# Graph message passing on one core: rows of x picked by TensorE in more steps, a third picked tile in every fourth step, and the edge bias put into PSUM by ScalarE

## The chip, the cores and the metric

The kernel runs on one core of a Trainium2 chip. The metric is the device time of one execution in microseconds (us); lower is better.

## The reference, cut to what matters

```python
# N = 6250 nodes, 64 channels, 4 heads of D = 16; 206250 edges, sorted by destination
Qh = (x @ Wq.T + bq).reshape(n, H, D)
Kh = (x @ Wk.T + bk).reshape(n, H, D)
Vh = (x @ Wv.T + bv).reshape(n, H, D)
Ee = (edge_attr @ We.T + be).reshape(-1, H, D)
score = (Kh[src] * Qh[dst] * (1.0 / np.sqrt(D)) * Ee).sum(-1)
score = jnp.exp(jnp.clip(score, -5.0, 5.0))
msg = Vh[src] * score[..., None]
wV = jax.ops.segment_sum(msg, dst, num_segments=n)
x = _layernorm(x + wV.reshape(n, H * D), axis=-1)
```

Two things are random access: the rows of K and V at `src`, and the rows of Q and of the output at `dst`. Since the edges are sorted by destination, the latter move slowly along the node axis; the sources are anywhere.

## The kernel before

**Tiling.** The edges are padded to 1612 tiles of 128. Eight tiles make a group (202 groups). The main loop has 105 steps: 97 of two groups (16 tiles), then eight of one group (8 tiles, the last 4). All tensors of a step lie with the edge of a tile on the partition.

**Prologue.** TensorE makes the tables: `kv_tab` (K and V of each node, f32, in HBM) and `q3_tab` (Q in three bf16 parts whose sum is the f32 value). The first four groups don't wait for `kv_tab`: GpSimd gathers rows of x (L230) and TensorE turns and multiplies them (L375 to L384). Then GpSimd starts gathering rows of `kv_tab`, one indirect DMA for each tile of 128 edges (L402, `gather_kv`), into one of five buffers `kvs`.

**Three ways to a K/V row.** Most tiles are gathered by L402. In each sixth step one tile comes by 128 single-row DMAs of the SP queue (L544, `rk`). And in steps 4 to 94 two tiles are *picked*: the last two tiles of the step after the next are made by TensorE. For a picked tile, ScalarE makes 50*column - source (`far`, L466), TensorE transposes it into the PSUM tile `small` (L471), VectorE compares that with block numbers and so makes 50 one-hot matrices of 128x128 in bf16 (`hot`, L481, in two halves of 25), and TensorE multiplies each with a block of `parts` (x in three bf16 parts; L491, 25 matmuls a half) and adds them up in PSUM (`pick`). VectorE adds the three parts (`xp`, L498), TensorE transposes, ScalarE copies, TensorE multiplies with the K and V weights (L513, L515), and ScalarE copies the result into `kvs` (L516). `parts` is made in the first steps of the loop from x in HBM, by `table_parts` and `table_parts_rest`.

**A step.** The schedule is written out by hand; each engine runs its instructions in program order. In step s, for step s+1: `spread` (L555) puts the destinations' offsets over the partitions, ScalarE makes one-hot rows `to` in two instructions (L572 Square, L577 Relu), `queries` (L595) multiplies them with the window of Q, `edges` (L388, L391) multiplies the edge attributes with their weights, and `onehot_edges` (L585) makes the one-hot columns. L388 is a matmul of three rows that starts each accumulation with the bias `be`, one for each group. For step s itself: two products on VectorE (L602 with Q, L603 with the edge values `pe`), the sum over each head (L609), the clip (L611), exp on ScalarE (L612), the message (L619). The message goes into three bf16 parts: ScalarE copies the first (L622), TensorE subtracts it in PSUM (L630, `minus`), ScalarE copies the next (L632), twice. For step s-1: `sums` (L638) multiplies the parts with the one-hot columns, and `add` (L652) adds the result to a ring of accumulators. When a block of 128 nodes is complete, in about every second step, VectorE closes it (L668 to L678), and later normalises it (L688). All the little PSUM tiles of a step (the turned sources, the scores, the sums) share the one tile `small`.

Of the kernel before, what the change touches and what calls it, by code (L numbers as in the profile page):

```python
# [40 lines left out]
TB = 8  # L41
M0 = 4
# [21 lines left out]
LAST = NS - 8 - 3  # L64


def picks_in(s):
    return M0 <= s <= LAST

# [5 lines left out]
COLUMN = 2 * G - 3  # L75
# [27 lines left out]
def tile_gnn(ctx: ExitStack, tc: tile.TileContext, x, xT, wT, bias, beT, weT, eT, src, dst, dst_rows,  # L103
# [52 lines left out]
    bkv_p = consts.tile([3, G // 2, 2 * C], BF16, name="bkv_p")  # L156
    minus_b = consts.tile([P, P], BF16, name="minus_b")
# [26 lines left out]
    with tc.tile_pool(name="nodes", bufs=1) as nodes, \  # L184
# [36 lines left out]
        nc.sync.dma_start(be_sb, beT.to_broadcast([3, C]))  # L221
        nc.vector.memset(we_sb, 0.0)
# [147 lines left out]
        for g in range(XG):  # L370
            for h in range(2):
                tp = npsum.tile([P, 2, P], F32, name="tp", bufs=2)
                for u in range(2):
                    j = 4 * h + 2 * u
                    nc.tensor.transpose(tp[:, u, :],  # L375
                                        XS[g][:, j:j + 2, :].rearrange("p j c -> p (j c)"), ident)
                xe = nodes.tile([P, 2, P], F32, name="xe", bufs=2)
                nc.scalar.activation(xe, tp, AF.Copy)
                pv = npsum.tile([P, 4, 2 * C], F32, name="pv", bufs=2)
                nc.tensor.matmul(pv, ones_b, bkv_p, start=True, stop=False, skip_group_check=True)  # L380
                for u in range(2):
                    nc.tensor.matmul(pv[:, 2 * u:2 * u + 2, :], xe[:, u, :], wkv, start=False,
                                     stop=u == 1, skip_group_check=True)
                nc.scalar.activation(kv_of(g)[:, 4 * h:4 * h + 4, :], pv, AF.Copy)  # L384

    def edge_values(pe, et, n):

        nc.tensor.matmul(pe[:, :n, :], ones_b, be_p[:, :n, :], start=True, stop=False,  # L388
                         skip_group_check=True)
        for u in range(n // 2):  # L390
            nc.tensor.matmul(pe[:, 2 * u:2 * u + 2, :], et[:, u, :], we_sb, start=False,  # L391
                             stop=u == n // 2 - 1, skip_group_check=True)
# [13 lines left out]
    for g in range(XG, 2 * KVB - 2):  # L406
        for j in range(G):
            gather_kv(g, j)
# [3 lines left out]
    with tc.If(rv == 0) as branch:  # L412

        with tc.tile_pool(name="work", bufs=2) as work, \
# [5 lines left out]
            col, from0, from1 = (small[:, i * C:(i + 1) * C].bitcast(BF16) for i in range(3))  # L420
            from_b = from0, from1
            score_all = small[:, 3 * C:3 * C + 2 * G * H]
            pa = small[:, 4 * C:7 * C].rearrange("p (i c) -> p i c", i=3)
            nc.tensor.transpose(col, row_b[:, 0:1].to_broadcast([P, P]), ident_b)

            parts = accp.tile([P, NB, 3, C], BF16, name="parts")
            nc.vector.memset(parts, 0.0)
            NX = N // NB
            x_v = x.rearrange("(p b) c -> p b c", p=NX)
            n_picks = LAST - M0 + 1  # L430
            src_f = accp.tile([P, n_picks, 2], F32, name="src_f")
            t0 = (M0 + 3) * 2 * G - 2
            for i in range(2):
                nc.vector.tensor_copy(src_f[:, :, i],
                                      src_i[:, t0 + i:t0 + i + 2 * G * (n_picks - 1) + 1:2 * G])
            pick = fixed.tile([P, 4 * P], F32, name="pick")
            rows3 = pick[:, :6 * C].rearrange("p (k i c) -> p k i c", k=2, i=3)
            HOT, FAR, X = {}, {}, {}
# [5 lines left out]
            def table_parts(b):  # L444

                n = min(TB, NB - b)
                raw = work.tile([P, TB, C], F32, name="raw", bufs=1)
                nc.sync.dma_start(raw[:NX, :n], x_v[:, b:b + n, :])
                rest = pick[:NX, :n * C].rearrange("p (b c) -> p b c", b=n)
                nc.scalar.activation(rest, raw[:NX, :n], AF.Copy)  # L450
                nc.scalar.activation(parts[:NX, b:b + n, 0], raw[:NX, :n], AF.Copy)
                return rest

            def table_parts_rest(b, rest):
                n = min(TB, NB - b)
                nc.vector.tensor_sub(rest, rest, parts[:NX, b:b + n, 0])
                nc.scalar.activation(parts[:NX, b:b + n, 1], rest, AF.Copy)
                nc.vector.tensor_sub(parts[:NX, b:b + n, 2], rest, parts[:NX, b:b + n, 1])

            def sources(s, i):  # L460

                if picks_in(s):
                    FAR[s, i] = work.tile([P, P], BF16, name="far")
                    nc.scalar.activation(FAR[s, i], row50, AF.Identity,  # L466
                                         bias=src_f[:, s - M0, i:i + 1], scale=-1.0)

            def sources_turned(s, i):
                if picks_in(s):  # L470
                    nc.tensor.transpose(from_b[i], FAR.pop((s, i)), ident_b)  # L471
# [4 lines left out]
            def hots(s, i, h):  # L476

                if picks_in(s):
                    HOT[s, i, h] = work.tile([P, NB // 2, P], BF16, name="hot", bufs=4)
                    shape = [P, NB // 2, P // 2, 2]  # L480
                    nc.vector.tensor_tensor(  # L481
                        HOT[s, i, h].rearrange("p b (a c) -> p b a c", c=2),
                        pairs(from_b[i])[:, None].to_broadcast(shape),
                        block2[:, blocks(h), None, :].to_broadcast(shape), op=OP.is_equal)

            def picks(s, i, h):
                if picks_in(s):
                    hot = HOT.pop((s, i, h))
                    for k in range(NB // 2):
                        b = h * NB // 2 + k  # L490
                        nc.tensor.matmul(rows3[:, i], hot[:, k, :], parts[:, b], start=b == 0,  # L491
                                         stop=b == NB - 1)

            def picked(s):

                if picks_in(s):
                    xp = work.tile([P, 2, C], F32, name="xp")
                    nc.vector.tensor_reduce(xp, rows3.rearrange("p k i c -> p k c i"), axis=AX.X,  # L498
                                            op=OP.add)
                    X[s] = xp  # L500

            def picked_turned(s):
                if picks_in(s):
                    room = psum.tile([P, G, P], F32, name="pb")
                    nc.tensor.transpose(room[:, 0, :], X[s].rearrange("p k c -> p (k c)"), ident)
                    xe = work.tile([P, P], F32, name="xe")
                    nc.scalar.activation(xe, room[:, 0, :], AF.Copy)
                    X[s] = xe, room[:, 4:6, :]

            def picked_kv(s):  # L510
                if picks_in(s):
                    xe, kv = X.pop(s)
                    nc.tensor.matmul(kv, ones_b, bkv_p[:, :2], start=True, stop=False,  # L513
                                     skip_group_check=True)
                    nc.tensor.matmul(kv, xe, wkv, start=False, stop=True, skip_group_check=True)  # L515
                    nc.scalar.activation(kvs[(s + 2) % KVB][:, 2 * G - 2:, :], kv, AF.Copy)  # L516

            def gather(s):
                for g in groups_of(s):
                    for j in range(tiles_of(g)):  # L520
                        if is_rowed(s) and (g - STEPS[s][0]) * G + j == COLUMN:
                            continue
                        if not picks_in(s - 2) or g == STEPS[s][0] or j < G - 2:
# [36 lines left out]
            def edges(s, k):  # L560

                g = STEPS[s][0] + k
                if k == 0:
                    PE[s] = psum.tile([P, 2 * G, C], F32, name="pe")
                edge_values(PE[s][:, k * G:(k + 1) * G], ET[g], tiles_of(g))
# [134 lines left out]
            closed, scaled, normed = 0, 0, 0  # L700
            keys(0)
# [5 lines left out]
            onehot_edges(0)  # L707
            for s in range(NS):
# [14 lines left out]
                sources_turned(s, 1)  # L723
                sources_turned(s + 1, 0)
                if nexts[1:]:
                    onehot_rows(nexts[1], spread(nexts[1]))
                making = [b for b in range(s * 2 * TB, (s + 1) * 2 * TB, TB) if b < NB]
                if making:
                    rest = table_parts(making[0])
                prod = products(s)  # L730
                picked(s - 1)
                if more:
                    edges(s + 1, 0)
                picks(s, 0, 0)
                score = scores(s, prod)
                if nexts[1:]:
                    onehot_rows_rest(nexts[1])
# [5 lines left out]
                picked_turned(s - 1)  # L743
                if nexts[1:]:
                    edges(s + 1, 1)
                minus(s, msg, 0)
                hots(s, 1, 0)
                picks(s, 0, 1)
                minus(s, msg, 1)
                picked_kv(s - 1)  # L750
# [4 lines left out]
                hots(s, 1, 1)  # L755
                picks(s, 1, 0)
                sources(s + 1, 1)
                sources(s + 2, 0)
                if s + 1 < NS:
# [6 lines left out]
                picks(s, 1, 1)  # L766
                hots(s + 1, 0, 0)
                hots(s + 1, 0, 1)
                if more:
# [13 lines left out]
                for i, b in enumerate(making):  # L783
                    if i:
                        rest = table_parts(b)
                    table_parts_rest(b, rest)
# [12 lines left out]
    with branch.Else():  # L799

        sums = [dram.tile([NR, C], F32, name=f"sums{i}") for i in range(TABLES)]
        with tc.tile_pool(name="gconsts", bufs=1) as gc, \
                tc.tile_pool(name="gloads", bufs=3) as loads, \
                tc.tile_pool(name="ggath", bufs=4) as gath, \
# [28 lines left out]
            def gather(g, j):  # L833
# [3 lines left out]
                if g >= 2 * KVB - 2:  # L837
# [11 lines left out]
            def compute(g):  # L849
# [33 lines left out]
                AGG[g] = work.tile([P, G, C], F32, name="agg", bufs=3)  # L883
# [79 lines left out]
```

## Time and profile before

| | |
|---|---|
| median of 3 runs | 1790.13 us (1790.07 to 1792.62) |
| profiled execution, its own time | 1789.88 us |
| its span, first to last instruction | 1788.0 us |
| mean granted TensorE clock | 0.951 |
| PE busy | 1638.5 us (92%) |
| VectorE (DVE) busy | 1481.6 us (83%) |
| GpSimd (POOL) busy | 1337.4 us (75%) |
| ScalarE (ACT) busy | 914.0 us (51%) |
| share of the chain that ended last | PE 38%, POOL 29%, issue 14%, DVE 13%, DMA 4% |

How to read the lines of the profile: a group's line has source line, engine, operation, output<-inputs, shapes and count, then busy us and mean ns of one, then the idle time of the engine ahead of them and what ended it. A timeline's line has start and duration in us, engine, line, operation and count, and in brackets the engine's idle time before it. A window's line has start:end, length, busy us (and instructions) of PE, PEld (weight loads), DVE, ACT and POOL, the granted TensorE clock, the DMA share and GB/s. POOL's busy time leaves out the 0.30 us between one gather and the next in which it issues. Matmuls are pipelined: the duration of one overlaps the next, so that the distance of starts is what a matmul costs.

### The profile page before, as it was taken

What the parts mean: (1) busy time and instruction counts of PE and PEld (TensorE: products, weight loads), DVE (VectorE), ACT (ScalarE), POOL (GpSimd) and SP (SyncE); (2) the same over time, 40 slices, a digit from 0 to 9 for tenths busy, and PEclk for the clock granted to TensorE, in tenths of its full rate; (3) what the DMA queues carried; (4) which work ended last, traced back from release to release, by engine and by line L of the source; (5) the groups of instructions that cost most, each with busy time, mean ns of one, the idle gap of its engine ahead of it and who ended that gap; (6) DMA issues with size and microseconds to landing.
All of it is one profiled execution on the core that took longest, in us unless ns stands there. A gap on an engine that the chain in (4) does not pass through costs nothing.

```text
span 1788.0 us, 44286 instructions
## 1 busy us (share of the span) xinstructions
PE 1638.5 (92%) x15751; PEld 1369.6 (77%) x15751; DVE 1481.6 (83%) x1695; ACT 914.0 (51%) x1328; POOL 1337.4 (75%) x1427
## 2 busy tenths in 40 slices
PE   8978999999999998999999899999989998999864
PEld 8647888888888787787887778777877887787632
DVE  6459999999998898888889888888988888898654
ACT  3465555555554464454455445455544554455443
POOL 7777777777777777777777777777777777777774
PEclk9968999999999999999999999999999999999855
DMA  7443333333333333332333333323332333333331
GB/s 221 132 121 84 90 93 94 93 94 92 93 81 94 93 86 89 92 94 80 93 93 81 93 81 93 92 81 99 87 93 80 94 93 81 93 90 81 91 80 44
DMA packets 109970, 166.71 MB, mean 93 GB/s; under 512 B 69196, under 2 KB 71452, under 8 KB 109626
## 3 DMA queue, kind: packets, MB, share of 16 engines
q0 software_dynamic: 45280, 91.78, 19.4%
q1 hardware_dynamic: 64074, 71.01, 14.1%
q8 instruction: 125, 2.05, 0.5%
q10 hardware_dynamic: 384, 1.00, 0.3%
q14 instruction: 107, 0.88, 0.2%
HBM read 156.33 MB, written 7.33 MB: 92 GB/s over the span
## 4 chain that ended last, share of the span: by engine, by line
PE 38%; POOL 29%; issue 14%; DVE 13%; DMA 4%; ACT 3%; DVEq 0%; SPq 0%; POOLq 0%; ACTq 0%
POOL kv L402 29%; PE pick L491 18%; PE pe L391 5%; DVE hot L481 5%; DMA kv<-kv_tab,src_i 3%; PE pq L630 2%; PE small L638 2%; DVE prod L603 2%; DVE prod L602 2%; PE pb L555 2%; PE pe L388 2%; PE pb L515 1%; PE pq L595 1%; DVE pq L619 1%; PE ps L350 1%
## 5 line engine op out<-in xcount | busy, mean ns | idle before, releaser
L402 POOL DMA_INDIRECT kv<-kv_tab,src_i x1383 | 1305.3, 944 | 421.7 <-issue 399.8
L491 PE MATMUL pick<-parts,hot 128*128 128x192 bf16 x9100 | 828.3, 249 | 0.0
L491 PEld LDWEIGHTS <-hot 128*128 128x128 bf16 x9100 | 771.7, 99 | 38.1
L481 DVE TENSOR_TENSOR hot<-small,block 128x3200 bf16<-128x3200 bf16 x364 | 645.3, 1813 | 0.4 <-PE pick L491 0.4
L572 ACT ACTIVATE to<-pb,minus_row 126x1024 bf16<-126x1024 f32 x202 | 222.7, 1102 | 371.0 <-PE pb L555 367.2
L632 ACT ACTIVATE msg<-pq 128x1024 bf16<-128x1024 f32 (+2 forms) x210 | 207.6, 989 | 222.3 <-PE pq L630 222.3
L391 PEld LDWEIGHTS pe<-we_sb,et 128*128 128x128 f32 x1612 | 209.7, 203 | 133.4 <-issue 95.3
L602 DVE TENSOR_TENSOR prod<-kv,pq 128x1024 f32<-128x1024 f32 (+2 forms) x105 | 123.5, 1176 | 169.3 <-DMA kv<-kv_tab,src_i 52.0
L391 PE MATMUL pe<-we_sb,et 128*128 128x128 f32 x1612 | 250.3, 302 | 0.0
L577 ACT ACTIVATE to<-to,one_p 126x1024 bf16<-126x1024 bf16 x202 | 230.6, 1142 | 3.5
L638 PEld LDWEIGHTS <-of 128*128 128x128 bf16 x1612 | 145.3, 102 | 31.1 <-issue 7.9
L638 PE MATMUL small<-msg,of 128*128 128x192 bf16 x1612 | 161.9, 257 | 0.5 <-ACT msg L632 0.5
L388 PE MATMUL pe<-be_p,ones_b 3*128 3x512 bf16 x202 | 79.7, 395 | 86.3 <-DVE prod L603 86.1
L630 PE MATMUL pq<-msg,minus_b 128*128 128x512 bf16 x404 | 128.0, 396 | 33.1 <-ACT msg L622 19.5
L622 ACT ACTIVATE msg<-pq 128x1024 bf16<-128x1024 f32 (+2 forms) x105 | 103.8, 989 | 96.8 <-DVE pq L619 96.8
L609 DVE TENSOR_REDUCE small<-prod 128x64 f32<-128x1024 f32 (+2 forms) x105 | 123.6, 1177 | 14.5 <-PE small L471 8.8
L555 PE MATMUL pb<-key_rows,ident_b 112*128 112x512 bf16 x403 | 127.9, 400 | 2.8 <-ACT to L572 2.8
L603 DVE TENSOR_TENSOR prod<-prod,pe 128x1024 f32<-128x1024 f32 (+2 forms) x105 | 123.6, 1177 | 3.6
L619 DVE TENSOR_TENSOR pq<-kv,small 128x1024 f32<-128x1024 f32 (+2 forms) x105 | 123.4, 1175 | 1.4 <-ACT small L612 1.4
L585 DVE TENSOR_TENSOR of<-small,key 128x2048 bf16<-128x2048 bf16 (+2 forms) x105 | 122.9, 1171 | 0.3
L595 PEld LDWEIGHTS <-to 126*128 126x128 bf16 x1612 | 63.5, 101 | 25.3 <-issue 25.1
L612 ACT ACTIVATE small<-small 128x64 f32<-128x64 f32 (+2 forms) x105 | 21.7, 207 | 111.1 <-DVE small L611 109.2
(129 smaller groups left out, 996.4 us busy)
## 6 DMA issues: line engine op xcount, KB each, us to landing
et<-in_eT SPq DMA_DIRECT2D x100, 512.0 KB
rk<-kv_tab SPq DMA_DIRECT2D x1920, 0.5 KB
kv<-kv_tab,src_i POOLq DMA_INDIRECT x1383
qw<-q_tab SPq DMA_DIRECT2D x202, 15.8 KB
kv_tab<-kv_sb SPq DMA_DIRECT2D x5, 640.0 KB
q_tab<-q SPq DMA_DIRECT2D x5, 480.0 KB
acc<-in_x SPq DMA_DIRECT2D x48, 32.0 KB
out<-y SPq DMA_DIRECT2D x48, 32.0 KB
```

The lines of the kernel that those rows point to most:

```text
L391: nc.tensor.matmul(pe[:, 2 * u:2 * u + 2, :], et[:, u, :], we_sb, start=False, stop=u == n // 2 - 1, skip_group_check=True)
L402: nc.gpsimd.indirect_dma_start(out=kv_of(g)[:, j, :], out_offset=None, in_=kv_tab[:, :], in_offset=bass.IndirectOffsetOnAxis(ap=src_i[:, t ...
L481: nc.vector.tensor_tensor(HOT[s, i, h].rearrange("p b (a c) -> p b a c", c=2), pairs(from_b[i])[:, None].to_broadcast(shape), block2[:, bl ...
L491: nc.tensor.matmul(rows3[:, i], hot[:, k, :], parts[:, b], start=b == 0, stop=b == NB - 1)
L555: nc.tensor.matmul(pb[:, b:b + 4, :], ident_b[:NR2, g // 2:g // 2 + 1].to_broadcast([NR2, P]), key_rows[:, g % 2, b * P:(b + 4) * P], star ...
L572: nc.scalar.activation(TO[g][:, :n, :], pb[:3 * W, :n, :], AF.Square, bias=minus_row3[:3 * W])
L577: nc.scalar.activation(TO[g][:, :n, :], TO[g][:, :n, :], AF.Relu, bias=one_p[:3 * W], scale=-1.0)
L602: nc.vector.tensor_mul(prod[:, :n, :], kvs[s % KVB][:, :n, :C], PQ[s][:, :n, :])
L603: nc.vector.tensor_mul(prod[:, :n, :], prod[:, :n, :], PE[s][:, :n, :])
L630: nc.tensor.matmul(msg[:, lo:hi, :], minus_b, M3[s][:, lo:hi, i, :], start=False, stop=True, skip_group_check=True)
L632: nc.scalar.activation(M3[s][:, :n, i + 1, :], msg[:, :n, :], AF.Copy)
L638: nc.tensor.matmul(PA[s], OH[s][:, j, :], M3[s][:, j], start=j == 0, stop=j == n - 1)
```

## The change

- Steps 0 to 96 pick a pair of tiles for the step two later, and steps 97 to 102 pick three more pairs, each over two steps and for the step three later (`PAIRS`, `TARGET`, `second_of`).
- In each fourth step from 0 to 92 a third tile is picked (`picks_third`, `i == 2`). Its one-hot halves are made ahead of and within the step, its matmuls go between the parts of the message, and it shares a PSUM region with the pair's second tile, which therefore comes after it, behind a reduction of its own (`picked_third`).
- The tile by SP moves from column 13 to 12 of its step.
- The edge bias is no longer a matmul in the loop: ScalarE copies `be_all` (the bias on all partitions) over the step's whole `pe` (`biases`), right behind exp, and the edge matmuls add to it. They move from before the first picks to behind them, and the second L577 moves behind them.
- `parts` is made in the prologue from `xT_sb`, which is on the chip: TensorE transposes, ScalarE copies, VectorE subtracts, between the pieces of the first groups' K and V, which are reordered so that the next transposes go ahead of the current products. The chunks of `table_parts` in the first steps go.
- The initial gathers leave out the five tiles that steps 0 and 1 pick. Buffers: `hot` 6 instead of 4, `far` 3 instead of 2.

The diff, cut to its core:

```diff
-LAST = NS - 8 - 3
+LAST = NS - 8 - 1
+PAIRS = [*range(LAST + 1), *range(LAST + 1, NS - 3, 2)]
+TARGET = {p: p + (2 if p <= LAST else 3) for p in PAIRS}
+def second_of(s):
+    return s if s <= LAST else s - 1 if s - 1 in PAIRS else None
+def picks_third(s):
+    return picks_in(s) and s % THIRD == 0 and STEPS[TARGET[s]][1] == 2
...
+        def parts_of_x(b):
+            n = min(TB, NB - b)
...
+            for u in range(n):
+                nc.tensor.transpose(px[:, u, :], xT_sb[:C, (b + u) * P:(b + u + 1) * P],
+                                    ident[:C, :C])
+            nc.scalar.activation(parts[:, b:b + n, 0], px, AF.Copy)
+            nc.vector.tensor_sub(px, px, parts[:, b:b + n, 0])
+            halves.append((px, b, n))
+        def rest_of_x():
+            px, b, n = halves.pop(0)
+            nc.scalar.activation(parts[:, b:b + n, 1], px, AF.Copy)
+            nc.vector.tensor_sub(parts[:, b:b + n, 2], px, parts[:, b:b + n, 1])
...
+        for i, gh in enumerate(order):
+            following = x_turned(*order[i + 1]) if i + 1 < len(order) else None
+            for b in blocks[2 * i:2 * i + 2]:
+                parts_of_x(b)
+            first_kv(*gh, xe)
+            xe = following
+            while halves:
+                rest_of_x()
...
-        nc.tensor.matmul(pe[:, :n, :], ones_b, be_p[:, :n, :], start=True, stop=False,
-                         skip_group_check=True)
+        if not biased:
+            nc.tensor.matmul(pe[:, :n, :], ones_b, be_p[:, :n, :], start=True, stop=False,
+                             skip_group_check=True)
...
+            def picked_third(s):
+                if picks_third(s):
+                    X[s] = work.tile([P, 3, C], F32, name="xp")
+                    nc.vector.tensor_reduce(X[s][:, 0], rows3[:, 1].rearrange("p i c -> p c i"),
+                                            axis=AX.X, op=OP.add)
...
+            def biases(s):
+                n = tiles_in(s)
+                nc.scalar.activation(pe_all[:, :n, :], be_all[:, None, :].to_broadcast([P, n, C]),
+                                     AF.Copy)
...
+            sources(0, 1)
+            sources(1, 0)
+            for i, h in ((0, 0), (0, 1), (2, 0)):
+                hots(0, i, h)
             for s in range(NS):
...
-                sources_turned(s, 1)
+                sources_turned(second_of(s), 1)
                 sources_turned(s + 1, 0)
+                sources_turned(s + 1, 2)
...
                 prod = products(s)
-                picked(s - 1)
-                if more:
-                    edges(s + 1, 0)
+                picked(second_of(s - 1))
                 picks(s, 0, 0)
                 score = scores(s, prod)
-                if nexts[1:]:
-                    onehot_rows_rest(nexts[1])
+                if more:
+                    biases(s + 1)
                 if s:
                     add(s - 1)
                 msg = message(s, score)
...
-                picked_turned(s - 1)
+                picked_turned(second_of(s - 1))
+                if more:
+                    edges(s + 1, 0)
                 if nexts[1:]:
                     edges(s + 1, 1)
+                    onehot_rows_rest(nexts[1])
                 minus(s, msg, 0)
-                hots(s, 1, 0)
+                hots(second_of(s), 1, 0)
+                hots(s, 2, 1)
                 picks(s, 0, 1)
+                picks(s, 2, 0)
                 minus(s, msg, 1)
-                picked_kv(s - 1)
+                picks(s, 2, 1)
+                picked_kv(second_of(s - 1))
...
-                hots(s, 1, 1)
-                picks(s, 1, 0)
+                hots(second_of(s), 1, 1)
+                if not picks_third(s):
+                    picks(second_of(s), 1, 0)
...
                     onehot_edges(s + 1)
                     queries(s + 1)
-                picks(s, 1, 1)
+                if not picks_third(s):
+                    picks(second_of(s), 1, 1)
                 hots(s + 1, 0, 0)
+                picked_third(s)
+                if picks_third(s):
+                    picks(second_of(s), 1, 0)
+                    picks(second_of(s), 1, 1)
                 hots(s + 1, 0, 1)
+                hots(s + 1, 2, 0)
```

## The prediction

> **What bounds the kernel now.** I read the share of each engine first, then the windows by stretch, then the timeline of single engines inside one step. "Step" is a pass of the main loop, "spread" its first matmul (L555), "prod" its first VectorE instruction (L602).
>
> The page's group for the gathers (count, busy, mean ns, idle before):
> ```profile
> L402 POOL DMA_INDIRECT kv<-kv_tab,src_i x1383 | 1305.3, 944 | 421.7 <-issue 399.8
> ```
> Busy and idle give 1727.0/1383 = 1.249 us per gather. The timeline has them on that beat from 43.04 to 1769.8 us without a hole, so POOL alone needs 43 + 1727 = 1770 us, and 18 us of last step follow. But the windows show two regimes (us, then busy PE, PEld, DVE, ACT, POOL, the granted clock, DMA):
> ```profile
> 300.00:500.00 200.00, 200.00 (x2097) 171.41 (x2095) 187.16 (x193) 109.93 (x154) 151.03 (x161) 1.00 0.34 92
> 900.00:1100.00 200.00, 187.83 (x1932) 160.71 (x1930) 172.10 (x176) 101.32 (x144) 151.23 (x161) 0.98 0.32 87
> ```
> Up to about 500 us PE has no hole: compute chases POOL, which started earlier. After that PE and DVE wait for rows. The distance of prods tells the two rates: 146.08 (step 4) to 506.50 (step 27) is 15.67 us a step; later POOL's 13.83 gathers a step make 17.27. So gathers are saved at 1.249 us each only while a step of compute stays below what POOL then needs. The reader should therefore look at the inside of an undisturbed step:
> ```profile
> 318.48 0.60 PE L555 MATMUL pb<-key_rows,ident_b 112*128 112x512 bf16 x2
> ...
> 320.88 0.39 PE L388 MATMUL pe<-be_p,ones_b 3*128 3x512 bf16 x1
> 321.19 1.16 PE L391 MATMUL pe<-we_sb,et 128*128 128x128 f32 x8
> 322.19 2.23 PE L491 MATMUL pick<-parts,hot 128*128 128x192 bf16 x25
> ...
> 334.12 0.60 PE L555 MATMUL pb<-key_rows,ident_b 112*128 112x512 bf16 x2
> ```
> Spread to spread 15.64 us (15.74 the step before), back to back: PE is full. ScalarE in the same step:
> ```profile
> 319.12 1.11 ACT L572 ACTIVATE to<-pb,minus_row 126x1024 bf16<-126x1024 f32 x1 [3.99 <-PE pb L555]
> 320.26 1.15 ACT L577 ACTIVATE to<-to,one_p 126x1024 bf16<-126x1024 bf16 x1
> 321.32 1.09 ACT L572 ACTIVATE to<-pb,minus_row 126x1024 bf16<-126x1024 f32 x1
> 322.31 0.21 ACT L612 ACTIVATE small<-small 128x64 f32<-128x64 f32 x1
> ```
> The exp starts 3.83 us after the spread, held by three ACT instructions, not by its data. And VectorE:
> ```profile
> 332.41 0.59 DVE L668 TENSOR_REDUCE y<-acc 128x64 f32<-128x256 f32 x1
> ...
> 333.91 1.22 DVE L602 TENSOR_TENSOR prod<-kv,pq 128x1024 f32<-128x1024 f32 x1 [0.29 <-DMA kv<-kv_tab,src_i]
> ```
> From exp to the end of the last hot is 332.41 - 322.31 = 10.10 us; the closing group adds 1.50 in about every second step; prod to exp is 302.52 to 306.90, 4.38.
>
> **The change, part by part.** Gathers: 100 pairs and 24 thirds are picked instead of 91 pairs, 224 tiles for 182. L402 falls by 42 to 1341, worth 42 x 1.249 = 52.4 us of POOL, whose last gather could end at 1718. That is the gain if nothing else is late.
>
> An ordinary step. The two L388 go (0.31 each, start to start: 0.62). In their place the bias is one ACT instruction right behind exp, and all edge matmuls now stand behind it and behind the first picks. No row shows a broadcast copy of 128x1024 f32 into PSUM; the nearest are L622 (0.99) and L577 (1.14); I take 1.0, for the shape of L622. PE reaches the edges at 0.44 + 1.32 + 0.11 + 0.53 (spread, sums, transposes, spread) + 2.06 (picks) + 0.21 (xp) = 4.67 after its spread; the bias ends at 3.83 + 0.15 + 1.0 + 0.04 = 5.02. So PE waits 0.35. Then 2.10 (edges) + 0.43 + 2.06 + 0.52 + 0.75 (kv) + 2.06 + 0.47 (queries) + 2.06 = 10.45: 15.47 us instead of 15.7. Over half of what the bias matmuls cost comes back as a wait. Queued behind bias on ACT are the first message part and the moved L577; the part is ready 3.17 after exp (322.31 to 325.49), and PE comes for it at 1.21 + 2.10 = 3.31, so that is covered, barely.
> If VectorE is late, exp follows prod by 4.38, so the edges start 5.59 after prod, and every us beyond prod = spread - 0.57 is PE idle. After a plain step prod is 13.93 - 15.47 = -1.54 (covered); after a closing group -0.04: 0.51 lost.
>
> A third. PE: 50 matmuls x 0.0824 = 4.12, plus 0.34 of small kv matmuls behind the edges: 4.46. VectorE: two hots of 1.73 and a reduction of 0.35. One of the hots (first half) is the last thing before the third's own step, so its prod comes at -1.54 + 1.73 = +0.19, or +1.69 with a closing group before. PE then has the first 25 picks only to fill the gap: edges at 5.78 or 7.28, and the step lasts 5.78 + 10.45 + 4.46 = 20.7, or 22.2. After it VectorE is early again (its reduction waits 0.4 us for the picks, PE's long pair follows), so nothing is carried on.
> Closing groups fall on odd steps 3 to 19 and 55 to 87, else on even ones, by the 62 rows a step moves; so 14 of the 24 thirds follow one. 96 steps: 72 x 15.47 + 10 x 20.7 + 14 x 22.2 + 22 x 0.51 = 1113.8 + 207.0 + 310.8 + 11.2 = 1643 us, 17.1 a step. POOL's new demand is 163 gathers per 12 steps, 16.96 us. So compute becomes the slower side and, starting behind, never catches up.
> PE at full load without any of these waits would take (15.74 - 0.62) + 4.46/4 = 16.24 a step; that is the lower end. With bias at 1.14 and VectorE always late by a closing group the step is 17.5, the upper.
>
> Prologue. Thirteen blocks of x: 52 transposes, and 4 ACT/DVE passes each that lie beside PE. Nearest row: L350, 55 matmuls in 11.85 us, 0.215 each: 11.2 us (5.7 if they ran at half of L505's 0.21, 14.8 at L375's 0.285). The x phase (51.7 to 77.0) is already solid on PE (26.33 of 27 us in 50 to 77), so they add to it, and the reordering there hides only a wait (0.51, L382 weights on ACT) that another matmul covers. Against that the memset (4.06) and the seven loop chunks of table_parts go; the memset lay beside PE. Ahead of step 0 come eight casts (0.15 each), then three hots on VectorE (5.2), of which about 2 show. First prod 84.97 + 11.2 + 2 = 98. Picks in step 0 start cold, +4 (25 picks at 3.62 rather than 2.23, three times).
>
> Tail. From the last double step's prod (1696.65) to the end are 91.4 us, of which 75 are POOL's beat. Now the gathers wait for nobody, but picks go on to step 102: step 97 repeats half a pair (`second_of(97)` is 96), steps 98 and 100 carry four hots (6.9 us behind the message, some 13 us a step), others stay near 9 (L602 at 1738.05, 1746.68, 1756.58). 13.5 + 11 + 13 + 9 + 13 + 9 + 9.5 + 8.5 + 14 = 100; 91 to 106 are the bounds.
>
> [...] In step 45 PE stood idle for 2.08 us and then ran 25 picks in 3.62 us at granted clock 0.66; after 2.85 us (at 1132.8) they kept 2.23. My 14 long thirds have gaps of 2.5 us, so they cost between 0 and 14 x 1.4 = 20 us more; I take none and keep 20 for the range. [...]
>
> **Sum.** 98 + 4 + 1643 - 1.5 (prod before spread) + 100 = 1843.5 span. The profiled run is 1789.88 for a span of 1788.0, and the median of the runs 0.25 above it: 1843.5 + 1.9 + 0.25 = 1845.7, say 1845.
>
> **Rivals.** (1) PE's own work is the bound, VectorE and bias stay covered, because the hots interleave better than I lay them out: 16.24 x 96 = 1559; 98 + 4 + 1559 + 100 + 2 = 1763, faster. It decides at 16.5 us a step, where 102 + 1584 + 100 + 2 = 1788. For it: PE shows no hole in 160 to 500 us. Against: the exp starts 0.23 us later than its clamp lets it already now (321.81 + 0.23 + 0.04 against 322.31), and thirds put 3.8 us on an engine at 94% (187.16 of 200). 15%. (2) POOL stays the bound and all 42 gathers count: 1790 - 52 = 1738; it needs a prologue and tail at no cost and 16.4 us a step. 4%. (3) The clock falls in the long thirds and bias takes 1.14: 1845 + 20 + 96 x 0.14 = 1878. 10%. (4) Gains and waits cancel: 1786.5 to 1793.5, 4%. That the change does not do what it says is small: the counts follow from the code, only the half pair in step 97 is made twice (8 us of PE and VectorE, in the tail above). My forecast has 67%.
>
> **Numbers.** 0.2% (3.6 us) is about what a measurement of this kernel can tell from no change. Faster: rivals 1 and 2, 0.19. Same: 0.04. Slower: 0.77. The range goes from rival 1 to rival 3, 1763 to 1880; the forecast's own is 1810 to 1870.
>
> **What would show it.** Right: L402 x1341 with POOL now waiting (for VectorE's message, which frees kv buffers); prods 15.5 us apart, then one of 20.7 to 22.2; edges (L391 before) waiting on the ACT bias; first prod near 98, the last double step's near 1743. Wrong: POOL still without a hole to 1718, or thirds under 20 us, or a mean step under 16.5.

## The result, and the profile after

The changed kernel takes 1842.57 us (median of 4 runs, 1833.30 to 1849.65), the kernel before 1790.16 (4 runs): ratio 1.0287, 95% interval 1.0236 to 1.0338. It is slower by 52 us; the forecast was 1845. The four runs fall into two pairs, 1833/1836 and 1849/1850, of which more below.

The profiled execution took 1835.83 us, its span is 1834.0. Its page, from the top (engine busy time and share, then the POOL row of the 40 slices, then groups with count, busy us, mean ns, idle before):

```profile
span 1834.0 us, 49044 instructions
PE 1720.3 (94%) x17906; PEld 1510.8 (82%) x17906; DVE 1640.9 (89%) x1832; ACT 1015.0 (55%) x1524; POOL 1298.3 (71%) x1385
POOL 7777777777777777777777777777777777775430
L458 POOL DMA_INDIRECT kv<-kv_tab,src_i x1341 | 1265.9, 944 | 466.8 <-issue 383.2
L540 PE MATMUL pick<-parts,hot 128*128 128x192 bf16 x11250 | 1003.2, 247 | 50.6 <-DVE xp L555 50.6
L635 ACT ACTIVATE pe<-be_all 128x1024 f32<-128x1024 f32 (+1 forms) x104 | 100.7, 969 | 0.0
```

L458 is the gather that was L402. The 42 gathers are gone, and POOL's idle time has grown: gathers and waits together are 1732.7 us, 5.7 more than before. The work has moved to PE (1638.5 to 1720.3 us busy) and VectorE (1481.6 to 1640.9). The waits answer for POOL says for whom it now waits (total us, times, longest):

```profile
POOL kv L458 <- DVE pq L690: 64.1, 21, 9.9
```

DVE L690 is the message product that frees a `kv` buffer: where POOL waits now, it waits for compute. In the middle of the run that is little. Cut to 150 to 1650 us, where the first of these waits ends at 1063.8 us, and to the time behind it, the same entry reads:

```profile
POOL kv L458 <- DVE pq L690: 15.6, 14, 3.3
POOL kv L458 <- DVE pq L690: 48.5, 7, 9.9
```

So compute is only a little slower than POOL in the loop, and three quarters of POOL's waiting lie behind 1650 us. PE's timeline in step 16, which picks a third (start, duration, line, operation, and in brackets the idle time before it):

```profile
350.48 0.60 PE L621 MATMUL pb<-key_rows,ident_b 112*128 112x512 bf16 x2
...
355.20 2.22 PE L540 MATMUL pick<-parts,hot 128*128 128x192 bf16 x25 [2.26 <-DVE xp L555]
...
357.78 2.05 PE L447 MATMUL pe<-we_sb,et 128*128 128x128 f32 x16 [0.25 <-ACT pe L635]
...
372.30 0.60 PE L621 MATMUL pb<-key_rows,ident_b 112*128 112x512 bf16 x2
...
388.29 0.60 PE L621 MATMUL pb<-key_rows,ident_b 112*128 112x512 bf16 x2
```

L621 is the spread, here of three steps in a row. The third's step lasts 372.30 - 350.48 = 21.82 us; the step behind it 15.99. The hole of 2.26 us stands ahead of the first picks, not ahead of the edges: the picks write the PSUM tile that VectorE's reduction L555 has still to read, and that reduction stands behind the late prod. PE's waits add up as follows over the whole run (total us, times, longest):

```profile
PE pick L540 <- DVE xp L555: 50.6, 37, 2.5
PE pe L447 <- ACT pe L635: 33.4, 95, 2.2
```

The second is the wait for the bias, 33.4/95 = 0.35 us each. VectorE around the hole of step 16:

```profile
345.52 5.27 DVE L530 TENSOR_TENSOR hot<-small,block 128x3200 bf16<-128x3200 bf16 x3
350.71 0.58 DVE L739 TENSOR_REDUCE y<-acc 128x64 f32<-128x256 f32 x1
352.21 1.22 DVE L673 TENSOR_TENSOR prod<-kv,pq 128x1024 f32<-128x1024 f32 x1 [0.29 <-issue]
354.60 0.55 DVE L555 TENSOR_REDUCE xp<-pick 128x128 f32<-128x384 f32 x1
```

Three hots instead of two and the closing group's reduction (L739) stand ahead of prod (L673), which starts 352.21 - 350.48 = 1.73 us after the spread, the step's own reduction behind it.

The first prod and that of the last double step (step 96), in the kernel before and in the changed one:

```profile
84.97 1.22 DVE L602 TENSOR_TENSOR prod<-kv,pq 128x1024 f32<-128x1024 f32 x1 [1.24 <-PE pq L595]
1696.65 1.22 DVE L602 TENSOR_TENSOR prod<-kv,pq 128x1024 f32<-128x1024 f32 x1 [7.05 <-ACT to L572]
78.86 1.22 DVE L673 TENSOR_TENSOR prod<-kv,pq 128x1024 f32<-128x1024 f32 x1
1723.87 1.21 DVE L673 TENSOR_TENSOR prod<-kv,pq 128x1024 f32<-128x1024 f32 x1
```

They split the 46.0 us between the two profiled spans: first prod 84.97 to 78.86 (-6.1), first prod to the last double step's prod 1611.7 to 1645.0 (+33.3), from there to the end 91.4 to 110.2 (+18.8).

### The profile page after: what moved, and what is told of

It is laid out like the page before. It is cut to its first block, busy times and chain, and to the rows that moved or that the text cites. A ratio compares the mean times of both kernels' runs of the same rounds, so it can differ in the third digit from the quotient of the medians.

```text
span 1834.0 us, 49044 instructions
## 1 busy us (share of the span) xinstructions
PE 1720.3 (94%) x17906; PEld 1510.8 (82%) x17906; DVE 1640.9 (89%) x1832; ACT 1015.0 (55%) x1524; POOL 1298.3 (71%) x1385
## 3 DMA queue, kind: packets, MB, share of 16 engines
q8 instruction: 142, 2.33, 0.5%
## 5 line engine op out<-in xcount | busy, mean ns | idle before, releaser
L458 POOL DMA_INDIRECT kv<-kv_tab,src_i x1341 | 1265.9, 944 | 466.8 <-issue 383.2
L540 PE MATMUL pick<-parts,hot 128*128 128x192 bf16 x11250 | 1003.2, 247 | 50.6 <-DVE xp L555 50.6
L540 PEld LDWEIGHTS <-hot 128*128 128x128 bf16 x11250 | 938.8, 98 | 125.3 <-issue 64.9
L530 DVE TENSOR_TENSOR hot<-small,block 128x3200 bf16<-128x3200 bf16 x450 | 797.5, 1813 | 0.0
L447 PE MATMUL pe<-we_sb,et 128*128 128x128 f32 x1612 | 210.4, 284 | 34.2 <-ACT pe L635 33.4
L447 PEld LDWEIGHTS pe<-we_sb,et 128*128 128x128 f32 x1612 | 190.7, 194 | 56.8 <-ACT pe L635 54.6
L709 PE MATMUL small<-msg,of 128*128 128x192 bf16 x1612 | 151.1, 247 | 1.0 <-DVE hot L530 0.5
L673 DVE TENSOR_TENSOR prod<-kv,pq 128x1024 f32<-128x1024 f32 (+2 forms) x105 | 123.1, 1172 | 30.1 <-ACT kv L582 10.7
L690 DVE TENSOR_TENSOR pq<-kv,small 128x1024 f32<-128x1024 f32 (+2 forms) x105 | 123.4, 1175 | 0.3 <-ACT small L683 0.3
L621 PE MATMUL pb<-key_rows,ident_b 112*128 112x512 bf16 x403 | 121.3, 381 | 2.4 <-ACT to L643 1.9
L635 ACT ACTIVATE pe<-be_all 128x1024 f32<-128x1024 f32 (+1 forms) x104 | 100.7, 969 | 0.0
L723 DVE SCALAR_TENSOR_TENSOR acc<-small,above,acc 128x192 f32<-128x192 f32 x103 | 43.0, 418 | 42.3 <-ACT small L683 41.0
L514 ACT ACTIVATE far<-row,src_f 128x128 bf16<-128x128 f32 x225 | 76.1, 396 | 0.7 <-DVE src_f L490 0.7
```

The costliest lines, as they stand in the source:

```text
L458: nc.gpsimd.indirect_dma_start(out=kv_of(g)[:, j, :], out_offset=None, in_=kv_tab[:, :], in_offset=bass.IndirectOffsetOnAxis(ap=src_i[:, t ...
L530: nc.vector.tensor_tensor(HOT[s, i, h].rearrange("p b (a c) -> p b a c", c=2), pairs(from_b[i])[:, None].to_broadcast(shape), block2[:, bl ...
L540: nc.tensor.matmul(rows3[:, min(i, 1)], hot[:, k, :], parts[:, b], start=b == 0, stop=b == NB - 1)
L673: nc.vector.tensor_mul(prod[:, :n, :], kvs[s % KVB][:, :n, :C], PQ[s][:, :n, :])
L690: nc.vector.tensor_mul(msg[:, :n, :].rearrange("p g (h d) -> p g h d", h=H), kvs[s % KVB][:, :n, C:].rearrange("p g (h d) -> p g h d", h=H ...
L709: nc.tensor.matmul(PA[s], OH[s][:, j, :], M3[s][:, j], start=j == 0, stop=j == n - 1)
```

## The experiments

The theory (A): with a third in one step of four, a step of compute is longer than POOL's new demand of 16.96 us, in part because the third's first hot makes VectorE late; besides, the picks in the last steps lengthen the tail. Rivals: (B) PE's wait for the bias on ScalarE is the cause; (C) it is the mere number of picks, a third costing its time wherever it stands. "Loop" is from the first prod to that of step 96.

**after_again**, the changed kernel once more, unedited.

> The changed kernel once more, as the neighbour of the three other kernels. All theories: 1833 to 1850. [...]

1848.73 us, ratio 1.0332 (1.0315 to 1.0350). The loop is the same, 1645.3 us; the first prod comes at 91.27 instead of 78.86. The spans of the two profiles, one near each pair of times, differ by 10.7 us, and that comes from the prologue; the long third steps whose picks are slow (25 in 3.09 to 3.87 us instead of 2.22 in the first profile) differ by one, four there and three here. PE's timeline of the prologue, the same four matmuls of the x phase, first in the earlier profile of the changed kernel:

```profile
52.80 2.08 PE L407 MATMUL pv<-wkv,xe 128*128 128x256 f32 x4
...
56.62 1.13 PE L407 MATMUL pv<-wkv,xe 128*128 128x256 f32 x4
```

and in after_again, where they keep 2.08 us to the end of the phase:

```profile
57.16 2.08 PE L407 MATMUL pv<-wkv,xe 128*128 128x256 f32 x4
...
79.13 2.08 PE L407 MATMUL pv<-wkv,xe 128*128 128x256 f32 x4
```

**no_thirds**, no third tiles; pairs, bias, tail and prologue stay.

```diff
 def picks_third(s):
-    return picks_in(s) and s % THIRD == 0 and STEPS[TARGET[s]][1] == 2
+    return False
```

> No third tiles; pairs from step 0 to the last steps, bias on ScalarE and prologue as changed: 1365 gathers. Theory A: a step of compute takes 15.5 to 15.7, below POOL's 17.3, so POOL is the bound again up to the last double step (43 + 1315 x 1.249 = 1685), and the tail of 105 to 110 us with its picks follows: 1790 to 1800. Rival B: the ScalarE bias still slows all steps: above 1800, compute-bound, POOL with holes. Rival C (only PE's matmul count matters): the same as theory A.

1798.64 us, ratio 1.0050 (1.0033 to 1.0066). The 24 thirds save 24 x 1.249 = 30 us of POOL and yet cost 50 us of time against after_again. Here the last double step's prod is at 1686.79, 9.9 us earlier than before, and the tail (109.7) gives more than that back.

**hot_inside**, the third's first hot made in the third's own step instead of at the end of the step before.

```diff
-            for i, h in ((0, 0), (0, 1), (2, 0)):
+            for i, h in ((0, 0), (0, 1)):
                 hots(0, i, h)
...
-                hots(second_of(s), 1, 0)
+                hots(s, 2, 0)
                 hots(s, 2, 1)
+                hots(second_of(s), 1, 0)
...
-                hots(s + 1, 2, 0)
```

> The third tile's first hot is made inside the third's own step instead of at the end of the step before. Theory A (VectorE is late by that hot, and PE stands idle behind it): the third step falls from 20.7 or 22.2 us to about 20.2, 96 steps from 1645 to about 1612, so 1800 to 1818. Rival B (the bias wait behind exp on ScalarE is what makes the loop slow): no change, 1833 to 1850. Rival C (PE's own added matmuls are): no change either.

1825.04 us, ratio 1.0186 (1.0161 to 1.0210); loop 1626.3, 19.0 less than in after_again with nearly the same first prod (92.53). Direction as in A, but little over half of the gain that A gave. PE's timeline of a third's step that no closing group precedes:

```profile
498.63 0.60 PE L621 MATMUL pb<-key_rows,ident_b 112*128 112x512 bf16 x2
...
503.65 2.05 PE L447 MATMUL pe<-we_sb,et 128*128 128x128 f32 x16 [0.38 <-ACT pe L635]
...
514.68 4.29 PE L540 MATMUL pick<-parts,hot 128*128 128x192 bf16 x50 [0.47 <-DVE xp L547]
...
518.80 0.60 PE L621 MATMUL pb<-key_rows,ident_b 112*128 112x512 bf16 x2
```

20.17 us with the hole ahead of the first picks gone, against 20.31 in the changed kernel for such a step. There the late hot costs next to nothing, since a new wait of 0.47 us (the pair's second tile behind the third's reduction, in the same PSUM region) takes its place. The gain is in the steps behind a closing group, 21.82 to 20.72 in most and 22.2 to 21.0 on average; 13 of the thirds stand there, and between 100 us and the loop's end no 25 picks take more than 2.24 us. And the loop's 1626.3/96 = 16.94 us is still POOL's demand of 16.96 within 0.02, so at best it ties with POOL. The late hot is a cause, of 19 us. What is left of the loop's length is PE's own work and its other waits, 54.8 us between 150 and 1650 us: 25.8 for the bias and 29.0 ahead of picks.

**bias_on_pe**, the bias matmuls back on PE, and the edges back where they were.

```diff
-                edge_values(PE[s][:, k * G:(k + 1) * G], ET[g], tiles_of(g), s > 0)
+                edge_values(PE[s][:, k * G:(k + 1) * G], ET[g], tiles_of(g))
...
                 picked(second_of(s - 1))
+                if more:
+                    edges(s + 1, 0)
                 picks(s, 0, 0)
                 score = scores(s, prod)
-                if more:
-                    biases(s + 1)
+                if nexts[1:]:
+                    onehot_rows_rest(nexts[1])
...
                 picked_turned(second_of(s - 1))
-                if more:
-                    edges(s + 1, 0)
...
-                    onehot_rows_rest(nexts[1])
```

> The bias is a matmul on PE again and the edge matmuls and the second Relu stand where they stood before; everything else as changed. Theory A: ordinary steps 15.74 instead of 15.47, third steps 20.6 or 22.1, so 96 steps take 1649 instead of 1645, and the time stays within 1835 to 1856. Rival B (the wait for the bias is the cause): the wait of about 1 us a step and more in the thirds goes, 16.3 a step, about 1770. Rival C: about 60 us of matmuls come back, 1895.

1866.16 us, ratio 1.0410 (1.0387 to 1.0434); loop 1663.5, 18.2 longer than in after_again, 0.19 a step: a plain step is back at 15.64 to 15.70, a step behind a third at 16.33 instead of 16.0. My range ended at 1856: moving the bias is worth more in this kernel than I gave it. B falls: the bias wait is not what made the kernel slower.

**before_bias**, the kernel before with the bias and the edges as changed, and nothing else.

```diff
-                if more:
-                    edges(s + 1, 0)
                 picks(s, 0, 0)
                 score = scores(s, prod)
-                if nexts[1:]:
-                    onehot_rows_rest(nexts[1])
+                if more:
+                    biases(s + 1)
...
                 picked_turned(s - 1)
+                if more:
+                    edges(s + 1, 0)
...
+                    onehot_rows_rest(nexts[1])
```

> The kernel before with one part of the change: ScalarE puts the bias into PSUM, and the edge matmuls stand behind the first picks. Theory A: steps 4 to 27, where compute has no holes, at 15.4 to 15.5 us instead of 15.67; the gathers still set the rest, total 1785 to 1792, no difference that counts. Rival B (PE's wait for the bias costs more than the two matmuls that it replaces): early steps 15.8 or more, total 1790 to 1800.

1790.10 us, ratio 1.0001 (0.9991 to 1.0011). The total is as expected, the early steps are not: 15.67 us, the same as before. Spread to spread, a plain step falls from 15.64 to 15.42, and a step behind a closing group rises from 15.74 to 15.97. There prod is late, the bias waits for exp, and the edges, which had stood ahead of it, wait for the bias. Half the early steps are of each kind, so the gain is nil. My own terms say so (15.47, and 0.51 lost behind a closing group); I left the second out of this expectation.

**no_tail**, pairs only in steps 0 to 94; thirds stay.

```diff
-LAST = NS - 8 - 1
-PAIRS = [*range(LAST + 1), *range(LAST + 1, NS - 3, 2)]
+LAST = NS - 8 - 3
+PAIRS = [*range(LAST + 1)]
...
-    return s if s <= LAST else s - 1 if s - 1 in PAIRS else None
+    return s if s in PAIRS else None
```

> The changed kernel with pairs only in steps 0 to 94, as before the change in its last steps; thirds, bias and prologue stay. 1351 gathers. Theory A (picks in steps 97 to 102 stretch the tail from 91 to 110 us, and steps 95 and 96 carry picks for them): tail 80 to 91 us, the last double step's prod some 4 us earlier, total 1803 to 1826, according to whether the first prod comes near 79 or near 91. Rival (the tail is set by its own chain of message, sums and normalisation, or by the gathers, not by picks): 1833 to 1850, as with the whole change.

1829.85 us, ratio 1.0223 (1.0206 to 1.0240), a little above my range, with the first prod at 91.92. The tail is 1825.5 - 1734.4 = 91.1 us instead of 108.1 in after_again: the picks of the last steps cost the 17 us, and their ten gathers saved nothing, since POOL is not the bound.

**third8**, a third in each eighth step, 12 instead of 24.

```diff
-THIRD = 4
+THIRD = 8
```

> The changed kernel with a third tile in every eighth step instead of every fourth: 12 thirds, 1353 gathers. Theory A (a third costs 5 to 6.5 us of compute, which shows only because 24 of them lift the mean step over POOL's): mean compute step 15.4 + (17.1 - 15.4)/2 = 16.3, under POOL's 13.71 x 1.249 = 17.12; so the gathers are the bound again, each of the 12 saves 1.249 us against no thirds at all: the last double step's prod near 1672, total 1780 to 1790. Rival (each third costs its time wherever it stands, half of 24 thirds costs half of what 24 cost): midway between 1799 and 1845, that is 1815 to 1828.

1788.90 us (10 runs), ratio 0.9992 (0.9982 to 1.0001): no difference from before, and 10 us below no thirds at all. C falls: half the thirds cost less than none. The last double step's prod is at 1673.22, 13.6 us earlier than in no_thirds, where 12 gathers less are 15.0. POOL is the bound again. The two largest entries of its waits from 150 to 1650 us are these, none longer than the 0.3 us that lie between any two gathers:

```profile
POOL kv L458 <- issue: 347.3, 1139, 0.3
POOL kv L458 <- DMA kv<-kv_tab,src_i: 8.2, 27, 0.3
```

The tail of 109.6 us, 18 longer than that of the kernel before, then takes most of the 23 us that were won up to there. The profiled run is the fastest of the ten, 1784.61 us; eight of them lie at 1788.2 to 1790.1, and no profile shows where those spend the 4 us more.

**before_reorder**, the kernel before with the x phase's new order only (the next transposes go ahead of the current products), one run.

> The kernel before with one part of the change: in the stage that makes K and V of the first groups from rows of x, the next transposes go ahead of the current products. Own theory of the prediction: it hides one wait of 0.5 us, PE's rate stays as it was (four L384 matmuls about 2.07 us), first prod 84 to 85. Rival (the order lets PE run this stage at its full rate, four matmuls 1.1 us, as in the changed kernel's second half of it): first prod 72 to 80. Total in both 1780 to 1792, as the gathers set the rest.

1789.92 us. First prod at 73.18, not the 84 to 85 that I expected: PE runs the phase at its full rate from 56.8 us on, as in the rival. But after_again has the same order and the slow rate throughout, 2.08 us for four matmuls, so the order alone does not decide it, and one run does not tell how often it helps. The 11.8 us are not in the total, since POOL sets it.

**mix6 and mix8**, what the runs point to: no picks behind step 94, the third's hot in its own step, a third in each sixth or eighth step.

```diff
-THIRD = 4
+THIRD = 6
```

In mix8 the new value is 8; the edits of hot_inside and no_tail are in both.

> The changed kernel with three edits: a third in every sixth step (16), its first hot made in its own step, and no picks behind step 94. Theory A: compute 15.4 + (16.95 - 15.4) x 4/6 = 16.4 us a step, POOL's demand 13.67 x 1.249 = 17.07, so all gathers count again: 1359 gathers end near 43 + 1359 x 1.249 = 1740, and 18 us follow as before: total 1755 to 1768, faster than both kernels. Rival (thirds and ScalarE's bias make a step dearer than 17.07 whatever their order): 1790 or more.

> As mix6 with a third in every eighth step (12). Theory A: compute has still more room (16.2 us a step), POOL has 4 gathers more: 1363 gathers end near 1745, total 1760 to 1772, that is 5 us above mix6. Rival (mix6 sits at the limit of compute, where late steps cost more than 4 gathers): mix8 below mix6.

3173.71 and 3163.00 us, where the kernel before took 3094.72 in the same comparison (ratios 1.0256 and 1.0218). Both were run again:

> The kernel of mix6 once more, since in the runs of that comparison TensorE waited some 0.7 us for single instructions in both kernels and all times were 1.7 times as long. Theory A as there: 1755 to 1768 where the kernel before takes 1790. Rival: 1790 or more.

> The kernel of mix8 once more, for the same reason. Theory A as there: 1760 to 1772, 5 us above mix6_again. Rival (mix6 sits at the limit of compute): below mix6_again.

3141.09 and 3134.15, where before took 3073.67 (ratios 1.0224, interval 1.0206 to 1.0241, and 1.0186, interval 1.0165 to 1.0206). In both comparisons, each on a chip that none of the other experiments ran on, the kernel before itself took 1.7 times as long as elsewhere. PE's timeline of mix6_again shows where, most of all at the query matmuls (516.5 us of idle time there that nothing in the profile ends, and 297.4 ahead of picks):

```profile
1009.14 2.23 PE L540 MATMUL pick<-parts,hot 128*128 128x192 bf16 x25
1012.70 0.53 PE L666 MATMUL pq<-qw,to 126*128 126x64 bf16 x7 [1.33 <-issue]
1014.47 0.19 PE L666 MATMUL pq<-qw,to 126*128 126x64 bf16 x1 [1.24 <-issue]
1015.21 0.21 PE L666 MATMUL pq<-qw,to 126*128 126x64 bf16 x1 [0.55 <-issue]
1017.30 0.21 PE L666 MATMUL pq<-qw,to 126*128 126x64 bf16 x1 [1.88 <-issue]
```

Matmuls come one by one, 0.7 us or a multiple of it apart, and wait for nothing that the profile shows; these picks ahead of them still run 25 in 2.23 us. A step takes 30.4 us. The times stand in the order of PE's matmul counts (15751 before, 16673 in mix8, 16889 in mix6), and neither theory is tested. Whether mix6 or mix8 beats the kernel before at 1790 us stays open; the parts of the sum were each measured apart (the tail in no_tail, POOL's bound in third8), the sum was not.

## Why the prediction was right, point by point

**Gathers and bound: right.** 1341 gathers; the 52.4 us on POOL are not in the time, POOL waits for VectorE's message, as said, though only 15.6 us of that lie between 150 and 1650 us.

**Ordinary step: right.** 15.47 predicted, 15.42 measured spread to spread; behind a closing group 15.98 predicted, 15.97 measured in before_bias. In the changed kernel these steps are not alike: 10 of 22 take 15.42, the others up to 17.15, on average 15.87. The bias instruction took 0.97 (1.0 taken).

**Third's step: right in mechanism and nearly in size.** Prod +0.19 and +1.69 us after the spread predicted, +0.23 and +1.73 measured; the step 20.7 and 22.2 predicted, 20.3 and 21.8 measured in most, 20.5 and 22.2 on average. 13 of them stand behind a closing group, not 14. The edges were to wait on the bias; the idle time came one place earlier, at the first picks, for the same late prod. "After it nothing is carried on" was wrong: the third's K and V matmuls, which I had put into the third's step (0.34), stand in the next, which takes 16.0. And it is the spreads that are 20 to 22 us apart; the prods, which I named as the sign, are 16 to 19 apart there (from step 15 to 18: 18.65, 16.86, 18.65), since the late prod shifts both of its distances.

**Loop: right in its total, in part by luck.** 1643 + 4 - 1.5 = 1645.5 predicted from the first prod to the last double step's, 1645.0 and 1645.3 measured. But the 95 steps behind step 0 took 5 us more than predicted (the steps behind thirds 12.5 more, thirds and ordinary steps 7 less), and step 0 took 19.0 us instead of 24.7. The 4 us for slow picks in step 0 were wrong: in the changed kernel none of them was slow, and in after_again only the first 25 were:

```profile
81.31 2.23 PE L540 MATMUL pick<-parts,hot 128*128 128x192 bf16 x25
94.09 3.68 PE L540 MATMUL pick<-parts,hot 128*128 128x192 bf16 x25
```

**Prologue: a term mis-sized.** The first prod was to come at 98 and came at 79 or 91. The step that failed is the price of the x phase: I took before's rate (2.07 us for four of its matmuls) for the rate of that code. The changed kernel runs the phase at that rate or, from some point in it on, at 1.13 for four. The added transposes were priced too high as well: 8 of them take 1.04 us start to start in after_again (0.13 each, 50 in all, so 6.5 us), not 0.215 each or 11.2.

**Tail: a term mis-sized.** 100 predicted (its nine steps add up to 100.5), 110.2 and 108.1 measured. Most of it lies in steps 96 (13.5 predicted, 16.0 measured), 98 (13, 16.2) and 102 (9.5, 11.4). That the gathers wait for nobody there was wrong, too: the 48.5 us that POOL waits for messages lie between 1674 and 1774 us, at the gathers for the steps of the tail. The errors of prologue and tail have opposite signs, so part of the total's closeness is luck: by the terms, 1843.5 = 98 + 4 + 1643 - 1.5 + 100; measured, 78.86 + 1645.02 + 110.17 = 1834.05 and 91.3 + 1645.3 + 108.1 = 1844.7.

**Rivals.** (1) failed by its floor, too. I put PE's work without those waits at 16.24 us a step; hot_inside, which takes most of the late hot away, has 20.17, 16.0, 15.42 and 15.42 where no closing group comes in between, 16.75 on average, and 16.94 over all. The 16.24 left out the bias wait (0.25 to 0.38 in each step) and the third's PSUM region (0.47 in each fourth), and with them the rival's deciding point of 16.5 was out of reach. (2) did not come: POOL had holes. In third8, with 12 thirds, it had none.

(3) rested on the clock, and the sum put that term at nothing, by a choice of mine that the runs do not bear out. Behind nine of the 13 long holes that follow a closing group the next 25 picks take 2.22 us, as in the row at 355.20; behind the other four they take 3.09 to 3.87 us, at a mean granted clock of 0.56 to 0.69 over these picks. The first of the four:

```profile
423.87 3.11 PE L540 MATMUL pick<-parts,hot 128*128 128x192 bf16 x25 [2.27 <-DVE xp L555]
425.02:428.43 3.41, 3.41 (x21) 3.33 (x20) 3.13 (x5) 2.17 (x4) 2.48 (x4) 0.50 0.18 44
```

Three of these steps take 22.73 to 22.81 us instead of 21.82 (the fourth is late for another reason, too), so I put the four at some 4 us, an estimate, of the 20 that I kept for them. The four stand behind holes of 2.26 to 2.33 us. In the kernel before, the slow picks of step 45 stand behind one of 2.08 us, with a granted clock of 0.50 from 820.62 to 824.04 us.

## What to carry to other kernels

When work moves from one engine to relieve another, price the whole step of the receiving engines against the new demand of the relieved one: here 24 thirds put compute at 17.1 us a step against POOL's 16.96, and 12 (third8) kept it below. An instruction that is made ahead at the end of a step delays the first instruction of the next chain on its engine; look at what stands last ahead of that, with the occasional work (the closing group) on top. And price the tail, where the old bound ends, by itself: picks that were carried on into the last steps cost 17 to 19 us here.

## What the runs showed of the hardware that was not expected

**The clock in the prologue.** The same four f32 matmuls take 2.08 or 1.13 us in one kernel's x phase. The rate changes where the clock records of a trace begin, with full clock: at 56.38 us in the changed kernel, 61.80 in third8, 56.17 in before_reorder. In after_again they begin only at 97.09 us and in the kernel before at 93.59, and there the whole phase stays at the slow rate. The views print a granted clock of 1.00 ahead of that because no record stands there; the 25 picks of after_again that start at 94.09 and take 3.68 us instead of 2.23 show that it was not so. So the two profiles of the changed kernel differ by the moment at which full clock was granted. What sets the moment was not found. It was not PE's load alone: in the kernel before PE was busy for 23.33 of the 24 us from 53 to 77, with transposes and matmuls at the slow rate.

**Which holes cost the clock.** The half-clock records in the changed kernel's loop last 3.41 us each and start whole multiples of that apart. Cut into stretches of that length, counted from the first record, the profile has PE idle for 2.1 to 2.8 us in the stretch just ahead of each of the four; in no other between 100 and 1690 us is it idle for more than 1.9 us (after_again: 2.2 to 2.4 ahead of its three, at most 1.9 elsewhere). The hole of 2.26 us in step 16 lies in two of these stretches, the one of 2.27 in step 20 in a single one (start:end, length, then PE's busy time):

```profile
349.93:353.34 3.41, 3.02 (x31) 2.38 (x29) 2.98 (x6) 2.19 (x3) 2.50 (x4) 1.00 0.45 75
353.34:356.75 3.41, 1.54 (x19) 1.54 (x19) 3.15 (x5) 1.24 (x4) 2.62 (x3) 1.00 0.60 201
421.61:425.02 3.41, 1.15 (x15) 1.15 (x14) 3.34 (x5) 1.46 (x2) 2.59 (x3) 1.00 0.74 215
```

So two holes of nearly the same length were followed by different clocks, 1.00 and 0.50. Other kernels went to half clock behind less: before, with 1.53 and 1.50 us of idle time in the stretches from 540.73 and 1196.09 us; in bias_on_pe, picks behind holes of 1.52 us take 3.63 to 3.88 us for 25 in four places and 2.23 in others. What decides was not found, and no run moved a hole on purpose.

**Single matmuls 0.7 us apart.** In the last two comparisons PE was held up, mostly at the query matmuls of a step, for no reason that the trace shows, and the kernel before took 3094.72 and 3073.67 us. What holds it up stays open.
